# Splitting the first block's scan and preparing modulated weights as columns in a one-core adaLN layer kernel

## The chip, the cores and the metric

The kernel runs on one core of a Trainium2 chip. The metric is the device time of one execution in microseconds. Each version is timed in several runs, and one further execution is recorded by the hardware profiler. All arithmetic is in float32.

## The reference, cut to what matters

```python
# x: (4, 2048, 512); c: (4, 512)
mod = (silu(c) @ wmod).reshape(4, 6, 1, 512)
sa, ca, ga, sb, cb, gb = mod[:, 0], mod[:, 1], ..., mod[:, 5]
ga = sign(ga) * max(|ga|, 0.25); gb = sign(gb) * max(|gb|, 0.25)     # sign(0) = +1
h = layernorm(x) * (1 + ca) + sa
x = x + ga * attn(h)
h = layernorm(x) * (1 + cb) + sb
x = x + gb * ffn(h)

# attn(u): M = 64, state of 2M per batch, scanned over t
omega = clip(softplus(u @ W_omega.T + b_omega), 1e-4, 100)
zeta = sigmoid(u @ W_zeta.T + b_zeta)
A = omega**2; S = 1 / (1 + DT*DT*A); d = 1 - zeta; F = u @ W_B.T + b_B
z[t] = d*(S*z[t-1] - DT*A*S*y[t-1]) + F[:M];  y[t] = d*(DT*S*z[t-1] + S*y[t-1]) + F[M:]
attn = concat(z, y) @ C.T + u @ D_mat.T

# ffn(x): x_prev is x one step earlier in t, 0 at t = 0
r = sigmoid((mu_r*x + (1-mu_r)*x_prev) @ W_r.T)
k = relu((mu_k*x + (1-mu_k)*x_prev) @ W_k.T)**2
ffn = r * (k @ W_v.T)
```

## The kernel before, in words

**Units and blocks.** Time is cut into eight blocks `s` of `W` = 256 steps. A unit is one batch of one block, so there are 32 units, numbered block by block: unit `i` has `s, b = divmod(i, 4)`. The order of the instructions on each engine is the order of the Python calls (`tc.manual_schedule()`); every engine works its own queue in that order, and semaphores make it wait for the others.

**Gates.** For each unit, `load` brings natural x into two tiles `xs` (three buffers in all), `norm` computes the layer-norm statistics with VectorE's BN instructions (`tile_stats`, L104, L105, L129) and the inverse deviation `rs` with a power on GpSimd (POOL, L130). `send` writes `rs` to DRAM and `spread` reads it back over all partitions as `bc`; the first four units do this with a diagonal matrix and a matmul instead (`spread_now`, L148 to L150). `project` (L161) multiplies the transposed x by a gate weight into the single PSUM buffer `pg`, and `hand_over` multiplies by `bc` (L169) and writes the gate inputs with four ScalarE instructions (L174) into `pre` and `f`.

**Scan.** `scan(s)` returns a list of steps with costs for all four batches of a block: softening (softplus and sigmoid by Abs, Exp and Ln on ScalarE, L191 to L194, then L200 to L205 on VectorE), eight chunk steps, six joins in a tree, the falls back down, eight state steps, and `by_batch`, which reorders the states and sends them to the tile `y` (L309). The list is taken a few steps at a time by `take(budget)` between other work. A chunk step begins with copies on ScalarE (L221 to L223).

**Finish.** For each unit, `attend` multiplies transposed x by `dg` (L347) and the states by `cg` (L348), adds both to x on VectorE (L350, L351), takes statistics and normalizes into `xn` (L363). `mix` transposes `xn` on TensorE (L382) and forms the two time-shifted mixtures on ScalarE and VectorE (L388, L391, and L394 on POOL for the first column). `key` (L407), `receptance` (L421) and `value` (L431) are the three products of the second half, with their results in PSUM buffers of the tag `pm` (two of them). The transposes use the two buffers of the tag `pt`, and attend's products the three of `px`.

**The loop.** Pass `i` of the main loop runs `key(i)`, the statistics of unit `i + 9`, `attend(i + 1)`, `receptance(i)`, `mix(i + 1)`, the gate products of unit `i + 8` and `value(i)`, and takes scan steps of the next block in between. So the gates of the first eight units and the whole scan of block 0 lie ahead of the loop.

**What is prepared ahead of the loop.** The six rows of the modulation are products with four output rows (`mod_rows`, L488); five of them are transposed into columns by `mod_cols` (L500, L501). From them come: gate weights `wgb`, centred by a matmul (`shared_weights`, L512, L517); `dg`, the D weights times ga along the output (`d_gate`, on POOL, L526), centred and scaled by `d_centre` (L533, L537); `cg`, the C weights times ga (L621, POOL); the row `d0`, spread through DRAM (`d_rows`, L505, L506) and added to x on POOL (`shift`, L337); and `wvb`, the value weights scaled by gb on ScalarE and transposed on TensorE, 16 pieces of 128 by 512 (`value_weights`, L670, L673, L674).

Transfers are issued by SP, apart from some weight loads that stand in ScalarE's queue.

Of the kernel before, what the change touches and what calls it, by code (L numbers as in the profile page):

```python
# [32 lines left out]

class Unit:
# [9 lines left out]
def adaln_layer_kernel(ctx: ExitStack, tc: tile.TileContext, x, x_t, c_t, wmod, w_gate, w_b, b_gate, b_f, c_mat, d_mat,  # L44
                       w_r, w_k, w_v, mu_r, mu_k, out):
# [12 lines left out]

# [25 lines left out]
    omus = const.tile([P, 2, KC], F32, name="omus")  # L84
    ct = const.tile([P, KC, B], F32, name="ct")
# [10 lines left out]
    def load_transposed(u):  # L96
        t = p3.tile([P, KC, W], F32, tag="xt", name=f"xt_{u.tag}")
        for n in range(NT):
            nc.sync.dma_start(t[:, :, ts(n, P)], x_t[u.b, u.t0 // P + n])
        return t  # L100
# [6 lines left out]
    pre_of, f_of, y_of = {}, {}, {}  # L107

    class Gates:
# [13 lines left out]
        def norm(self):  # L123
# [8 lines left out]
        def send(self):  # L132
            self.row = dram.tile([W], F32, tag=f"st{self.u.tag}", name=f"st_{self.u.tag}")
            nc.sync.dma_start(self.row.rearrange("(n p) -> p n", p=P), self.r)

        def load_t(self):
            self.xt = load_transposed(self.u)

        def spread(self):
            self.bc = p2.tile([P, W], F32, tag="bc", name=f"bc_{self.u.tag}")  # L140
            nc.sync.dma_start(self.bc, self.row.unsqueeze(0).broadcast_to([P, W]))

        def spread_now(self, diag):
# [3 lines left out]
            for n in range(NT):  # L147
                nc.vector.tensor_scalar_mul(diag[:, ts(n, P)], ident, self.r[:, n : n + 1])  # L148
                nc.tensor.matmul(pb[:, ts(n, P)], ones, diag[:, ts(n, P)], start=True, stop=True)
            nc.scalar.copy(self.bc, pb)  # L150

        def project(self):
            u = self.u
            s, b = u.s, u.b
            if s not in pre_of:
                pre_of[s] = p2.tile([P, 2, L, Q, NCH], F32, tag="pre", name=f"pre_{s}")
                f_of[s] = p2.tile([P, 2, L, Q, NCH], F32, tag="f", name=f"f_{s}")
# [7 lines left out]
        def hand_over(self):  # L165
            u = self.u
            s, b = u.s, u.b
            g = p1.tile([P, 2, W], F32, tag="g", name=f"g_{u.tag}")
            nc.vector.tensor_mul(g, self.pg, self.bc.unsqueeze(1).broadcast_to([P, 2, W]))  # L169
            q, hs = b // 2, slice((b % 2) * M, (b % 2) * M + M)  # L170
            for i, dst in enumerate((pre_of[s], f_of[s])):
                for j in range(2):
                    src = slice(j * M, j * M + M)
                    nc.scalar.activation(  # L174
                        dst[hs, j, :, q, :].rearrange("p l c -> p c l"),
                        g[src, i, :].rearrange("p (c l) -> p c l", l=L),
                        AF.Identity,
                        bias=bias[src, i, b : b + 1],
                    )

    def scan(s):


        env = {}

        def soften_act():
            pre = env["pre"] = pre_of[s]
            env["f"] = f_of[s]
            o, z = (pre[:, j].rearrange("p l q c -> p (l q c)") for j in range(2))
            t = env["t"] = p1.tile([P, Q * W], F32, tag="soft", name=f"soft_{s}")  # L190
# [5 lines left out]
        def soften(lo, hi):  # L196

            pre, t = env["pre"], env["t"][:, lo:hi]
# [8 lines left out]
        def at(name, kind, l):  # L207
            return env[name][:, kind, l].rearrange("p q c -> p (q c)")

        def both(l):  # L210
            return env["f"][:, :, l].rearrange("p i q c -> p i (q c)")
# [3 lines left out]
        def chunk_step(l):  # L215


            new = p2.tile([P, 2, 3, QC], F32, tag="new", name=f"new_{s}_{l}")
            gl, al = at("pre", 0, l), at("pre", 1, l)
            if l == 0:  # L220
# [8 lines left out]
            uv = p1.tile([P, 2, 3, QC], F32, tag="uv", name=f"uv_{s}_{l}")  # L229
            gv = p1.tile([P, 3, QC], F32, tag="gv", name=f"gv_{s}_{l}")  # L230
# [3 lines left out]
                al.unsqueeze(1).broadcast_to([P, 6, QC]),  # L234
# [380 lines left out]
    for b in range(2):  # L615
        d_gate(b)
# [182 lines left out]
```

## Time and profile before

| quantity | value |
|---|---|
| median of 3 runs | 1261.17 us (1259.66 to 1262.08) |
| the profiled execution | 1261.01 us |
| its span, first to last instruction | 1259.2 us |
| mean granted TensorE clock | 0.958 |
| PE, PEld, DVE, ACT, POOL busy | 1160.7, 674.8, 752.0, 477.7, 174.4 us |
| share of the span in the chain that ended last: PE, DVE, ACT, DMA | 86%, 3%, 2%, 2% |

PE is TensorE's matmul, PEld its weight loads, DVE VectorE, ACT ScalarE, POOL GpSimd, SP the engine that issues most transfers. A float32 matmul is recorded as two passes: four matmuls into one tile stand as `x8`. The chain of waits is followed back from the last instruction: each piece of time is put down to the instruction that the next one had to wait for. The granted clock is the share of full speed that TensorE was given.

### The profile page before, as it was taken

To read this page: it belongs to the slowest core of one execution; us is meant where nothing else is said; L and a number is where in the kernel's file an instruction comes from. 1 tells how busy PE (TensorE), PEld (TensorE's weight loads), DVE (VectorE), ACT (ScalarE), POOL (GpSimd) and SP (SyncE) were. 2 spreads that over 40 slices of the span, in tenths; PEclk is the share of its full clock that TensorE was granted. 3 is DMA by queue.
4 is the path that set the end of the run, shared out by engine and by line. 5 is a ranking of instruction groups with operands and counts; after the bars stand their busy time and mean duration, and the time that the engine had idled before them with its cause. 6 is when DMAs were issued, how large, how long until landed. Compare 5 with 4: busy or idle time off the path is not lost.

```text
span 1259.2 us, 11785 instructions
## 1 busy us (share of the span) xinstructions
PE 1160.7 (92%) x3692; PEld 674.8 (54%) x3692; DVE 752.0 (60%) x2044; ACT 477.7 (38%) x796; POOL 174.4 (14%) x254
## 2 busy tenths in 40 slices
PE   6781475899999999999999999999999999999998
PEld 2621343456655566555665555665556665555554
DVE  2557513886488647874587538863886368743332
ACT  1331534333453345434533445334533453233232
POOL 0340001111101111111111111110111011111110
PEclk9895667899999999999999999999999999999999
DMA  8565423123333333233322232323232211121100
GB/s 266 194 118 93 74 67 79 39 80 88 104 89 88 88 87 85 88 89 96 89 81 68 75 95 80 88 88 105 88 89 71 67 50 51 51 67 50 50 18 33
DMA packets 120270, 105.95 MB, mean 84 GB/s; under 512 B 15880, under 2 KB 90120, under 8 KB 119952
## 3 DMA queue, kind: packets, MB, share of 16 engines
q1 hardware_dynamic: 116064, 101.27, 29.7%
q10 hardware_dynamic: 4144, 3.94, 1.0%
q8 instruction: 29, 0.48, 0.2%
q14 instruction: 33, 0.27, 0.1%
HBM read 84.16 MB, written 16.82 MB: 80 GB/s over the span
## 4 chain that ended last, share of the span: by engine, by line
PE 86%; DVE 3%; ACT 2%; DMA 2%; issue 1%; POOL 0%; SPq 0%; DVEq 0%; ACTq 0%
PE pk_c L407 18%; PE pr_c L421 18%; PE pv_c L431 17%; PE pd_c L347 17%; PE pg L161 8%; PE pc_c L348 4%; PE pt_c L382 2%; PE pwv L673 1%; DMA bc<-st 1%; DMA xs<-in_x_dram 1%; PE pdm L533 1%; ACT wvs L670 1%; ACT wvb L674 1%; ACT f L174 0%; ACT pre L174 0%
## 5 line engine op out<-in xcount | busy, mean ns | idle before, releaser
L407 PE MATMUL pk_c<-mixed_c,wk 128*128 128x256 f32 x1024 | 228.1, 381 | 12.9 <-POOL mixed_c L394 12.9
L347 PE MATMUL pd_c<-dg,xt 128*128 128x512 f32 x512 | 232.4, 597 | 0.0
L421 PE MATMUL pr_c<-wr,mixed_c 128*128 128x512 f32 x512 | 227.0, 596 | 0.0
L431 PE MATMUL pv_c<-wvb,act_c 128*128 128x512 f32 x512 | 225.0, 592 | 0.0
L407 PEld LDWEIGHTS pk_c<-mixed_c,wk 128*128 128x128 f32 x1024 | 195.7, 191 | 53.3 <-issue 14.8
L391 DVE SCALAR_TENSOR_TENSOR mixed_c<-pt_c,prev_f,mixed_c 128x255 f32<-128x255 f32 x256 | 118.1, 482 | 122.9 <-ACT mixed_c L388 122.9
L363 ACT ACTIVATE xn_c<-x,nmr_c,rstd_c 128x512 f32<-128x512 f32 x64 | 48.6, 805 | 334.6 <-POOL nmr_c L360 334.6
L421 PEld LDWEIGHTS pr_c<-wr,mixed_c 128*128 128x128 f32 x512 | 98.2, 192 | 123.9 <-issue 123.8
L347 PEld LDWEIGHTS pd_c<-dg,xt 128*128 128x128 f32 x512 | 98.1, 192 | 110.6 <-issue 108.8
L431 PEld LDWEIGHTS pv_c<-wvb,act_c 128*128 128x128 f32 x512 | 96.7, 190 | 108.9 <-issue 106.2
L350 DVE SCALAR_TENSOR_TENSOR x<-pd_c,rs,x 128x512 f32<-128x512 f32 x64 | 47.5, 743 | 169.0 <-PE pd_c L347 168.9
L161 PE MATMUL pg<-xt,wgb 128*128 128x256 f32 x512 | 121.0, 391 | 15.4 <-DVE g L169 15.4
L388 ACT ACTIVATE mixed_c<-pt_c,mod,now_f 128x256 f32<-128x256 f32 x256 | 130.4, 561 | 11.9 <-DVE mixed_c L391 5.6
L412 ACT ACTIVATE act_c<-pk_c 128x512 f32<-128x512 f32 x64 | 38.2, 597 | 202.2 <-PE pk_c L407 202.2
L161 PEld LDWEIGHTS pg<-xt,wgb 128*128 128x128 f32 x512 | 98.7, 197 | 29.1 <-DVE g L169 15.5
L433 DVE TENSOR_TENSOR r_c<-pv_c,r_c 128x512 f32<-128x512 f32 x64 | 44.2, 690 | 90.8 <-PE pv_c L431 88.8
L359 POOL TENSOR_TENSOR rstd_c<-rstd_c,neg_half 128x2 f32<-128x2 f32 x32 | 24.6, 769 | 515.9 <-DVE nmr_c L358 515.9
L174 ACT ACTIVATE pre<-g,bias 64x256 f32<-64x256 f32 x64 | 46.8, 731 | 84.8 <-DVE g L169 84.3
L337 POOL TENSOR_TENSOR x<-x,d 128x1024 f32<-128x1024 f32 x32 | 75.6, 2362 | 2.0 <-DMA x<-in_x_dram 2.0
L348 PE MATMUL pc_c<-cg,y 128*128 128x512 f32 x128 | 66.4, 601 | 4.8 <-DVE x L350 4.8
L130 POOL TENSOR_TENSOR rs<-var,neg_half 128x2 f32<-128x2 f32 x32 | 24.9, 779 | 306.8 <-DVE var L129 292.1
L423 ACT ACTIVATE r_c<-pr_c 128x512 f32<-128x512 f32 x64 | 36.9, 588 | 51.1 <-PE pr_c L421 51.0
(119 smaller groups left out, 1029.6 us busy)
## 6 DMA issues: line engine op xcount, KB each, us to landing
xt<-in_x_t_dram SPq DMA_DIRECT2D x128, 256.0 KB, 4.6
xs<-in_x_dram SPq DMA_DIRECT2D x64, 256.0 KB, 4.6
x<-in_x_dram SPq DMA_DIRECT2D x32, 512.0 KB, 4.0
out_dram<-r_c SPq DMA_DIRECT2D x64, 256.0 KB, 2.1
wvb<-in_wmod_dram SPq DMA_DIRECT2D x5, 1024.0 KB, 9.5
y<-pre SPq DMA_DIRECT2D x64, 64.0 KB, 2.0
bc<-st SPq DMA_DIRECT2D x28, 128.0 KB, 4.7
wvb<-in_wmod_dram SPq DMA_DIRECT2D x4, 256.0 KB, 4.7
```

Of the source, the lines that this page charges most:

```text
L161: nc.tensor.matmul(self.pg[:, i, :], wgb[:, b, k, ts(i, P)], self.xt[:, k, :], start=(k == 0), stop=(k == KC - 1))
L174: nc.scalar.activation(dst[hs, j, :, q, :].rearrange("p l c -> p c l"), g[src, i, :].rearrange("p (c l) -> p c l", l=L), AF.Identity, bias ...
L337: nc.gpsimd.tensor_tensor(xt, xt, d0[:, self.u.b, :].unsqueeze(1).broadcast_to([P, NT, D]), ALU.add)
L347: nc.tensor.matmul(pd, h[:, k, ts(n, P)], dg[:, b, k, :], start=(k == 0), stop=(k == KC - 1))
L348: nc.tensor.matmul(pc, y_of[u.s][:, b, ts(n, P)], cg[:, b, :], start=True, stop=True)
L350: nc.vector.scalar_tensor_tensor(xt[:, n, :], pd, r, xt[:, n, :], ALU.mult, ALU.add)
L363: nc.scalar.activation(self.xn[:, n, :], xt[:, n, :], AF.Identity, bias=nmr[:, n : n + 1], scale=rstd[:, n : n + 1])
L388: nc.scalar.activation(m, pt, AF.Identity, bias=mod[:, 2, k, b : b + 1], scale=now_f[:, b, i, k : k + 1])
L391: nc.vector.scalar_tensor_tensor(m[:, 1:], pt[:, : W - 1], prev_f[:, b, i, k : k + 1], m[:, 1:], ALU.mult, ALU.add)
L407: nc.tensor.matmul(pk[:, j, :], wk[:, k, ts(2 * e + j, P)], mixed[:, 1, k, :], start=(k == 0), stop=(k == KC - 1),)
L421: nc.tensor.matmul(pr, mixed[:, 0, k, ts(n, P)], wr[:, k, :], start=(k == 0), stop=(k == KC - 1))
L431: nc.tensor.matmul(pv, act[:, k, ts(n, P)], wvb[:, u.b, k, :], start=(k == 0), stop=(k == KC - 1))
```

## The change

Block 0 is scanned in two parts, batches 0 and 1 first and batches 2 and 3 later; `part` gives each its half of `pre` and `f`, and `scan(0, 0)` and `scan(0, 1)` are two lists with instructions of half the width. The other blocks are scanned as before. The order ahead of the loop and in its first four passes is written anew: the loop now starts with five units' gates done, and the gates of units 5 to 11 are computed in passes 0 to 3. The five modulation vectors after ca come directly as columns (`mod_cols`, 16 small matmuls). D is loaded in its natural layout and scaled in three places: `d_scaled` multiplies it by the ca row on VectorE, `Turn.rows` by the ga column on ScalarE with the centring as a bias, and `Turn.turn` transposes it on TensorE, with copies back by `keep`. C and the value weights take the same way. The statistics of the units from 2 on are two accumulating ScalarE instructions per tile, and units 2 to 7 send and spread `rs` from POOL's queue. For block 0, `d0` is added inside the states' PSUM group by a matmul that picks the row (`states`). The first units' x is loaded once for Gates and Finish, and free weight tiles hold it meanwhile. In pass 3 receptance and value come ahead of the next unit's attend.

```diff
+    def part(s, q):
+        if s not in parts_of:
...
+            if s == 0:
+                n = 2 * L * NCH
+                parts_of[s] = [Part(s, h, 1, pre[:, ts(h, n)], f[:, ts(h, n)]) for h in range(Q)]
+            else:
+                parts_of[s] = [Part(s, 0, Q, pre, f)] * Q
+        return parts_of[s][q]
-        def norm(self):
+        def norm_dve(self):
...
+        def norm(self, junk=False):
...
+                nc.scalar.activation(t, src, AF.Identity, scale=-1.0 / D, accum_out=mean[:, n : n + 1])
...
+                nc.scalar.activation(
+                    t, src if junk else t, AF.Square, scale=1.0 if junk else -float(D), bias=mean[:, n : n + 1],
+                    accum_out=var[:, n : n + 1],
+                )
+            nc.gpsimd.tensor_scalar(var, var, 1.0 / D, EPS, ALU.mult, ALU.add)
+            nc.gpsimd.tensor_tensor(self.r, var, neg_half, ALU.pow)
-        def hand_over(self):
+        def multiply(self):
+            self.g = p1.tile([P, 2, W], F32, tag="g", name=f"g_{self.u.tag}")
+            nc.vector.tensor_mul(self.g, self.pg, self.bc.unsqueeze(1).broadcast_to([P, 2, W]))
+        def deliver(self, share=False):
...
+                    if share and i == 1:
+                        nc.vector.tensor_scalar_add(there, here, bias[src, i, b : b + 1])
+                    else:
+                        nc.scalar.activation(there, here, AF.Identity, bias=bias[src, i, b : b + 1])
-    def scan(s):
+    def scan(s, q=0):
+        to = part(s, q)
...
+        def states(self, n):
+            pc = ps3.tile([P, D], F32, tag="px", name=f"pc_{self.tag}_{n}")
+            if self.row is not None:
+                pick = ident[:B, u.b : u.b + 1].broadcast_to([B, P])
+                nc.tensor.matmul(pc, pick, self.row, start=True, stop=False)
+            nc.tensor.matmul(pc, y_of[u.s][:, u.b, ts(n, P)], cg[:, u.b, :], start=(self.row is None), stop=True)
...
+    def mod_cols(wm, name):
+        pt = ps2.tile([P, KC, B], F32, tag="pt", name=name)
+        for e in range(KC):
+            for k in range(KC):
+                nc.tensor.matmul(pt[:, e, :], wm[:, k, ts(e, P)], st[:, k, :], start=(k == 0), stop=(k == KC - 1))
+        return pt
+    def d_scaled(b):
+        pc = ps3.tile([P, D], F32, tag="px", name=f"pca{b}")
+        pick(pc, carow[:B, :], b)
+        nc.vector.tensor_mul(dg[:, b], dn, pc.unsqueeze(1).broadcast_to([P, KC, D]))
+    class Turn:
+        def rows(self):
+            for e in range(KC):
...
+                    nc.scalar.activation(
+                        a, self.src[:, e, :], AF.Identity, scale=self.scale[:, e, b : b + 1],
+                        bias=self.shift[:, e, b : b + 1],
+                    )
+        def turn(self):
+            self.pts = [
+                ps2.tile([P, D], F32, tag="pt" if k < 2 else "pm", name=f"turn_{self.name}{self.b}_{k}")
+                for k in range(KC)
+            ]
+            for k, pt in enumerate(self.pts):
+                for e in range(KC):
+                    nc.tensor.transpose(pt[:, ts(e, P)], self.dst[:, e, ts(k, P)], ident)
+        def keep(self):
+            for k, pt in enumerate(self.pts):
+                nc.scalar.copy(self.dst[:, k, :], pt)
+    weights_to(dn, d_mat, nc.scalar)
+    weights_to(dt, d_t, nc.scalar)
+    weights_to(cn, c_mat, nc.scalar)
+    weights_to(wn, w_v, nc.scalar)
...
+    gts[1].deliver(share=True)
+    side += scan(0, 0)
+    take(0.1)
+    d_scaled(0)
+    d_scaled(1)
+    take(3.4)
...
+    shared_weights(3, pws[1])
+    fin[0].add_products()
+    turn_v[0].rows()
+    turn_d[1].turn()
+    turn_d[1].keep()
+    turn_c[1].turn()
+    turn_c[1].keep()
+    d_scaled(2)
+    fin[0].attend(lambda: None)
+    gts[2].project()
...
+    fin[0].mix(lambda: None)
+    gts[4].project()
+    turn_v[0].turn()
+    gts[3].deliver()
+    side += scan(0, 1)
+    take(0.1)
+    turn_v[0].keep()
+    gts[4].multiply()
+    gts[4].deliver()
+    gts[6].norm()
...
+        if i == 0:
+            gates(5)
+            gts[6].spread(nc.gpsimd)
+            gts[7].norm()
+            gts[7].send(nc.gpsimd)
+            gts[8].load()
+            gts[8].norm()
+            gts[8].send()
+            turns = [turn_d[2], turn_c[2]]
+        if i == 1:
+            take(1)
+            gates(7)
...
+            turns = [turn_d[3], turn_c[3], turn_v[1]]
+        if i == 2:
+            gates(9)
+            fin[4].load()
+            turns = [turn_v[2]]
+        for t in turns:
+            t.rows()
...
+        if late:
+            take(1)
+            f.receptance()
+            turn_v[3].turn()
+            turn_v[3].keep()
+            ahead.products()
+            gates(11)
+            ahead.add_products()
+            f.value(lambda: None)
+            ahead.attend(lambda: None)
+            ahead.mix(fin[i + 2].shift)
...
+            if ahead:
+                ahead.attend(lambda: take(a2))
+            if i == 1:
+                side += scan(1)
+                take(0.1)
+            take(b_)
+            for t in turns:
+                t.turn()
+                t.keep()
+            f.receptance()
```

## The prediction

> **What bounds the kernel now.** I read the busy rows of the page first, then the windows by stage, then the chain of waits, then the timeline at the places where the chain leaves TensorE.
>
> ```profile
> PE   6781475899999999999999999999999999999998
> PEclk9895667899999999999999999999999999999999
> 0.00:36.58 36.58, 24.29 (x84) 10.98 (x84) 9.68 (x31) 3.52 (x6) 2.10 (x8) 0.95 0.86 283
> 91.99:162.80 70.81, 22.71 (x84) 16.54 (x84) 43.66 (x149) 24.62 (x42) 7.08 (x16) 0.60 0.44 74
> 204.57:251.58 47.01, 42.20 (x117) 23.86 (x118) 32.70 (x78) 15.61 (x28) 7.36 (x9) 0.89 0.28 75
> 285.13:318.68 33.55, 33.55 (x109) 19.83 (x109) 19.93 (x60) 13.91 (x24) 4.52 (x7) 1.00 0.32 83
> ```
>
> In the PE row only the first eight slices are not full. In a window the columns are length, then busy time of PE, PEld, DVE, ACT and POOL, then granted clock, DMA share and GB/s. From the second pass on, PE is busy 33.55 of 33.55 us: nothing is to be had there unless TensorE gets less work. The loss is all ahead of that.
>
> ```profile
> 204.57 8.90 PE pk_c L407 x32
> 251.58 6.91 PE pk_c L407 x32
> 285.13 6.91 PE pk_c L407 x32
> 318.68 6.91 PE pk_c L407 x32
> 352.23 6.91 PE pk_c L407 x32
> ```
>
> These are the starts of key(0) to key(4) in the chain. After key(4) both versions have the same work left (gates of units 12 on, passes 4 to 31), so I ask one thing: when does key(4) start? The gain is 352.23 minus that.
>
> ```profile
> 36.58 0.68 DVE L169 TENSOR_TENSOR g<-pg,bc 128x512 f32<-128x512 f32 x1
> 67.94 1.28 ACT L192 ACT_TABLE_LOAD   x1
> 69.24 0.63 ACT L192 ACTIVATE soft<-soft 128x512 f32<-128x512 f32 x1
> 90.01 0.69 DVE L104 BATCH_NORM_STATS2 stats_a<-xs 128x6 f32<-128x512 f32 x1 [10.79 <-DMA xs<-in_x_dram]
> 91.99 0.41 DVE L200 SCALAR_TENSOR_TENSOR pre<-pre,soft 128x256 f32<-128x256 f32 x1
> 162.80 5.01 SPq L309 DMA_DIRECT2D y<-pre  x8
> 172.90 5.83 PE L347 MATMUL pd_c<-dg,xt 128*128 128x512 f32 x8
> 204.57 8.90 PE L407 MATMUL pk_c<-mixed_c,wk 128*128 128x256 f32 x32 [12.93 <-POOL mixed_c L394]
> ```
>
> First gate product 36.58, first softening on VectorE 91.99 (after four gates and a 10.79 us wait for xs), states sent 162.80, key(0) 204.57. The eight pd_c passes took 5.83 us there, 3.43 in the steady chain: a cold start, 2.4 us.
>
> **The change, by stages up to key(4).** Durations are rows of before. (a) *To the first product.* mod_rows (3.43 us at full clock) becomes mod_cols: 32 passes with 4 columns; L601 did 16 such passes in 1.84 us, so 3.7: no gain each. But only two pw (1.99 each) and one mod stand ahead: pw to 17.8, wgb to 19.4, diagonal and its matmul 20.7, psa 24.5, bias matmuls 26.7, pg 3.7, so product at 30.5 (was 36.58). ScalarE issues four weight loads here and stays behind their queue slots until about 25 (the first window moves 283 GB/s; some 6.5 MB stand up to the D load, 23 us); its next work, bc, is needed only at 30: cost 0, up to 6 if that cover is gone.
>
> (b) *To softening.* Gate 1: 35.5. Its f half on VectorE: no row; bounds 0.29 (a plain 128x256 tensor_scalar) and 0.74 (the strided twin on ScalarE), taken 0.4 each. Two d_scaled, 128x2048: four L351 rows make 2.8, without their starts 2.1; taken 2.3. Softening at 40.8 (was 91.99). It no longer waits for gates 2 and 3, for centring or for xs.
>
> (c) *To the states.* Softening 3.7; gate columns seven small ones, 1.4: 46.0. The first chunk step then waits for three copies on ScalarE behind D rows (four L670 rows at 0.70) and C rows (4 x 0.29): 50.5. Half-width steps: 1.31 for 1.85 (128x192 0.36, 128x96 0.26 and so on); seven of them and two small copies 60.0; joins 3.0, start 0.8, five falls 3.1, eight state steps at 0.98 (was 1.18), gb 1.0: 75.7. States are sent at 76.4 (was 162.80). ScalarE's statistics of units 2 to 4 (eight and four L413-like rows of 0.63) and TensorE's column products lie beside it.
>
> (d) *To key(0).* VectorE wgb and products 4.8 (80.5); ScalarE copy, statistics 5, V rows, first keep 83.0; turned C and pick, cold, 85.7; d_scaled 2.3; attend sums to 92.0; POOL 0.95, xn 1.6, gates 3, pick and transposes to 99.9; mixed to 105.5. Then a **new wait**: turn_v[0] takes both "pm" PSUM buffers, and ScalarE empties them only after deliver(3) 2.95, softening 4.0 with two table loads, and three keeps 1.7: key(0) at 113.7 (was 204.57). Behind key(0) on TensorE stands gate 5, and VectorE's product 5 stands ahead of the second scan, which so starts at 126.8.
>
> (e) *Pass 0, 61.2 us (was 47.0).* Key cold 8.9, gate 5 3.45, product 0.7; ScalarE deliver 2.95, statistics 7 and 8 5.1, wait for xs of unit 8 about 3 (its buffer is freed inside statistics 7, landing 4.6), D and C rows 4.0, copies 0.6: 142.6. VectorE step, first tile, step, second tile 7.5; POOL and xn 2.5; D keeps 1.7: 154.3, when receptance gets its buffer; cold 9.1, transposes 1.0, gate 6 3.5, value 6.9: key(1) at 174.9.
>
> (f) *Pass 1, 65.3 (was 33.55).* The second scan ends at 189.0, its states land 193.6 (four issues 0.63 apart, 2.0 us landing); attend cold to 202.3; sums, POOL, xn 4.4, softening of block 1 5.0, eight keeps 4.5: 216.2; receptance cold 9.1, four d0 picks 3.4, transposes 1.1, gate 8 3.5, value 6.9: key(2) at 240.2 (was 285.13).
>
> (g) *Pass 2, 50.0.* Key and gate 9 10.4; product, four full steps, tile, step, tile 15.0; POOL and xn 2.5, keeps 1.7; receptance cold 8.9, transposes, gate, value 11.5: key(3) at 290.2. (h) *Pass 3, 48.6.* Scan of block 1 ends 304.8, copies and sigmoid 3.2, turns 0.6, products 6.9, gate 11, value, states 12.1; then with TensorE empty sums 3.2, POOL 1.0, xn 1.5, transposes 1.1, half of mixed 2.4, a cold start 2: key(4) at 338.8.
>
> **Sum:** 352.23 - 338.8 = 13.4. The profiled execution took 1261.01 us with a span of 1259.2, 0.16 under the median of the runs, 1261.17. 1261.0 - 13.4 = 1247.6, say 1248.
>
> **Costed at nothing.** In the steady passes 1.9 us of VectorE (two L104, two L105, L129) become 2.55 of ScalarE, which is busy 13.91 of 33.55; it runs under the 8.6 us of attend products. Uncovered it would cost 2.55 x 20 units = 51. An accumulating ACTIVATE has no row: at least the plain 0.63, at most one more small instruction (0.22) each; I take the plain one, 20 on the chain, so up to 4. The st and bc transfers of units 2 to 7 move from SP's queue to POOL's, which SP's loads no longer stand behind; before showed 8.0 and 4.7 us to landing on SP. On POOL they may be some us later or earlier; unit 6 has 40 us to spare, unit 4 about 4. On SP the two bounces of ga and d0 through DRAM (L505, L506) and 2.5 MB of second loads for block 0 go, and 1 MB of D transposed comes. W_k and W_r move from ScalarE's queue to SP's: W_k stands ahead of nothing needed before 60 us, W_r is issued at about 101 and is first read at 154. Transposed x of units 4 to 7 now goes into wvb, so these issues wait on SP for the sb and gb columns (about 55 and 65), with only xs of unit 5 and the y transfers (76) behind them: 11 us of cover, and each us beyond it is a us of key(0). What POOL loses is large: D and C products of 2391 ns x8 and 1288 x4, and their contention; no gain counted beyond the stages.
>
> **Two rules that speak against it.** Pass (d) to (f) put transposes where the centring matmuls were. The Trainium skill, TensorE: Matmul & The Clock Gate (Part 4: PE-mode transpose; Why this matters for your kernels), says that transposes do not count as TensorE activity for its clock, and that gaps of some 3 us bring half rate. The pd_c row agrees: it began slow right after 16 us of transposes. With its 2.4 at most I put some 14 us of cold starts into (d) to (h); by the page, half of a 3.4 us window, 1.7 each, they would be 12. The other rule, ScalarE: Activation LUTs (What ACT_TABLE_LOAD costs), charges 2.66 us for a switch; here the load at 67.94 was over in 1.28 and the next instruction began at 69.24. Four loads on the chain would cost 5.5 more by the page; I keep the trace's.
>
> **Rivals.** *A, the queues close up.* Passes 0 to 3 hold only 165 us of TensorE work at full clock (4 x 30.1, seven gates 24.2, 88 transposes 11.4, ten picks 8.6) against my 225. If a third of the 60 us of waits and cold starts is not there, key(4) is at 319 and the time 1228. For it: I let every wait end last in full. Against: the queues are in order and the buffers few. *B, TensorE stays cold* (slower). Place: passes 0 to 2, 129 us of work at full clock, 142 with my cold starts, a mean clock of 0.91. The windows of before had 0.60 to 0.70 where PE was half busy, and 0.89 at 42.20 of 47.01. At 0.80 the 129 become 161: 19 more, time 1267. It turns slower once the clock of these passes is below about 0.83 and the stretch lies on the chain. Against: most of the waits there are for ScalarE, and some stretch hides under them. *C, statistics* of 1.4 us instead of 0.63 on ScalarE would eat the gain; nothing near that is in the trace.
>
> **How the numbers follow.** Forecast 0.54 (1248, own range 1236 to 1260); A 0.18 (1228); B 0.24 (1267); C 0.04 (1265). The measurement tells 0.2%, 2.5 us, from no change. Forecast, about seven eighths, and A are faster: 0.65; the rest of the forecast and the lower edge of B are the same: 0.09; slower 0.26. The range reaches from the lower side of A to the upper of B, 1224 to 1271.
>
> **What would show it.** Right: first product near 30, states sent near 76, key(0) near 114 ended by ScalarE's keep and not by POOL, key(2) near 240 and key(4) near 339, then 33.55 us per pass. Wrong: a steady pass above 33.6 (statistics uncovered); a clock under 0.83 in passes 0 to 2 (B); L178 or L180 above 0.85 us (C); first product after 36 (loads hold ScalarE).

## The result, and the profile after

The changed kernel takes 1265.71 us (median of 7 runs, 1261.14 to 1269.88) against 1261.17 for the kernel before on the same chip (7 runs, 1259.66 to 1262.59): ratio 1.0033, 95% interval 1.001 to 1.0056. The forecast was a gain of 13 us; it lost 4.5. Its profiled execution took 1264.29 us with a span of 1262.3, 1.4 under its median.

The busy rows of the page after, in 40 slices of 31.6 us:

```profile
PE   6998688789889999999999999999999999999998
...
PEclk8677888898989999999999999999999999999999
```

PE is fuller at the start than before, and its clock lower in the first three slices (8, 6, 7 for 9, 8, 9), higher in the four behind them. The windows of the changed kernel by the stages of the forecast (length; busy PE, PEld, DVE, ACT, POOL; clock; DMA share; GB/s):

```profile
0.00:37.04 37.04, 26.61 (x99) 18.94 (x100) 8.56 (x30) 3.94 (x6) 2.09 (x8) 0.82 0.99 321
37.04:47.66 10.62, 10.21 (x58) 8.08 (x57) 7.56 (x8) 6.88 (x13) 0.00 (x0) 0.95 0.65 240
47.66:89.74 42.08, 41.17 (x184) 35.33 (x185) 28.27 (x139) 19.71 (x49) 9.14 (x25) 0.65 0.52 107
89.74:131.18 41.44, 28.61 (x106) 17.57 (x104) 17.59 (x32) 25.05 (x46) 4.34 (x10) 0.80 0.44 70
131.18:189.62 58.44, 47.91 (x148) 29.03 (x149) 24.64 (x77) 36.08 (x75) 7.02 (x15) 0.85 0.15 37
189.62:256.89 67.27, 53.74 (x173) 31.84 (x172) 33.06 (x115) 40.02 (x73) 3.21 (x9) 0.87 0.26 67
```

The third row is the odd one. TensorE is busy 41.17 of 42.08 us, yet its granted clock is 0.65. The timeline of the changed kernel shows the work (start, length, instruction, times; in brackets the idle time ahead of it and who ended it):

```profile
21.12 5.37 PE L617 MATMUL psa<-st,wvb 128*128 128x4 f32 x32
26.75 3.57 PE L752 MATMUL pbias<-mod,wraw 128*128 128x4 f32 x16 [0.27 <-DVE mod L742]
30.19 6.75 PE L218 MATMUL pg<-xt,wgb 128*128 128x256 f32 x16
37.04 0.69 DVE L224 TENSOR_TENSOR g<-pg,bc 128x512 f32<-128x512 f32 x1 [6.12 <-PE pg L218]
...
47.25 6.97 PE L617 MATMUL pga<-st,wvb 128*128 128x4 f32 x32
54.07 6.97 PE L617 MATMUL pcb<-st,wvb 128*128 128x4 f32 x32
54.25 0.17 DVE L623 TENSOR_SCALAR sgna<-pga 128x16 f32<-128x16 f32 x1 [2.81 <-PE pga L617]
72.76 0.17 DVE L805 COPY mod<-psb 128x16 f32<-128x16 f32 x1 [3.62 <-PE psb L617]
79.27 3.63 PE L617 MATMUL pgb<-st,wvb 128*128 128x4 f32 x32
131.18 9.20 PE L513 MATMUL pk_c<-mixed_c,wk 128*128 128x256 f32 x32 [6.15 <-ACT wvb L684]
```

One vector of 32 passes with 4 columns takes 3.63 at 79.27, 113 ns a pass, and 6.97 at 47.25 and 54.07, 218 ns. The first is the price the forecast used for all five. The gate product at 30.19 takes 6.75 where the next one takes 3.72. TensorE does not idle in either; it works at half clock, as the windows over these instructions show (the gate product, the cb vector, the gb vector):

```profile
30.19:36.80 6.61, 6.61 (x18) 5.30 (x19) 0.56 (x3) 0.00 (x0) 0.00 (x0) 0.53 1.09 356
54.07:61.00 6.93, 6.93 (x34) 6.93 (x35) 2.19 (x13) 4.47 (x11) 1.05 (x3) 0.50 0.55 28
79.30:82.80 3.50, 3.50 (x35) 3.50 (x33) 3.05 (x18) 3.33 (x10) 0.02 (x1) 1.00 0.01 2
```

Against the forecast, from the start of the span:

| | before | forecast | after |
|---|---|---|---|
| first gate product | 36.58 | 30.5 | 37.04 |
| first softening on VectorE | 91.99 | 40.8 | 47.66 |
| states sent | 162.80 | 76.4 | 89.74 |
| key(0) | 204.57 | 113.7 | 131.18 |
| key(1) | 251.58 | 174.9 | 189.62 |
| key(2) | 285.13 | 240.2 | 256.89 |
| key(3) | 318.68 | 290.2 | 307.49 |
| key(4) | 352.23 | 338.8 | 352.61 |

In this trace all of the miss lies ahead of key(0): 6.5 us to the first product, 6.5 from the softening to the states (42.1 for 35.6), 4.1 from there to key(0). The four passes took 221.4 for 225.1. At key(4) the kernels are level; key(4) begins at half clock behind a wait of 2.10 us for POOL (it takes 9.44 for 7.07), so that key(5) is 2.9 us late (388.69 against 385.79), and that is nearly all of the 3.1 by which the span is longer.

Executions differ. The run e6_stats below has the same instructions up to pass 3. In its trace the sb vector ran mostly at full clock, VectorE did not wait for it, and the stage from the softening to the states was shorter, 39.43 for 42.08:

```profile
47.36:86.79 39.43, 38.58 (x184) 32.51 (x184) 28.22 (x139) 19.72 (x49) 9.16 (x25) 0.67 0.56 115
65.86 3.91 PE L619 MATMUL psb<-st,wvb 128*128 128x4 f32 x32
```

Its key(0) starts at 127.26 and its key(3) at 301.38, 3.9 and 6.1 us ahead of the trace above, with nothing changed. So a difference of a few us between two single traces shows no effect of an edit by itself; there the medians and their intervals decide.

### The profile page after: what moved, and what is told of

Same layout as the page of the kernel before. It is cut to its first block, busy times and chain, and to the rows that moved or that the text cites. A ratio compares the mean times of both kernels' runs of the same rounds, so it can differ in the third digit from the quotient of the medians.

```text
span 1262.3 us, 12427 instructions
## 1 busy us (share of the span) xinstructions
PE 1194.8 (95%) x3896; PEld 716.6 (57%) x3896; DVE 703.7 (56%) x2000; ACT 583.9 (46%) x1092; POOL 153.5 (12%) x282
## 4 chain that ended last, share of the span: by engine, by line
PE 72%; issue 0%; DVE 0%; POOL 0%; DVEq 0%; POOLq 0%
PE pk_c L513 16%; PE pv_c L537 15%; PE pr_c L527 15%; PE pd_c L420 15%; PE pg L218 5%; PE pc_c L446 4%; PE pt_c L488 2%; DVE r_c L539 0%; DVE r_c L540 0%; POOL mixed_c L500 0%; POOL edge_c L480 0%; DVEq L539 0%; POOLq L413 0%
## 5 line engine op out<-in xcount | busy, mean ns | idle before, releaser
L513 PE MATMUL pk_c<-mixed_c,wk 128*128 128x256 f32 x1024 | 231.3, 384 | 9.7 <-ACT wvb L684 6.1
L469 ACT ACTIVATE xn_c<-x,nmr_c,rstd_c 128x512 f32<-128x512 f32 x64 | 48.6, 806 | 270.5 <-POOL nmr_c L466 270.5
L218 PE MATMUL pg<-xt,wgb 128*128 128x256 f32 x448 | 106.9, 394 | 1.2 <-DVE g L224 1.2
L218 PEld LDWEIGHTS pg<-xt,wgb 128*128 128x128 f32 x448 | 87.2, 199 | 15.0 <-DVE g L224 1.8
L446 PE MATMUL pc_c<-cg,y 128*128 128x512 f32 x128 | 69.8, 630 | 3.1 <-DMA y<-pre 3.1
L413 POOL TENSOR_TENSOR x<-x,d 128x1024 f32<-128x1024 f32 x28 | 65.9, 2355 | 0.0
L184 POOL TENSOR_SCALAR var<-var 128x2 f32<-128x2 f32 x30 | 5.8, 192 | 431.9 <-ACT xs L180 411.1
```

The source lines that it names most:

```text
L218: nc.tensor.matmul(self.pg[:, i, :], wgb[:, b, k, ts(i, P)], self.xt[:, k, :], start=(k == 0), stop=(k == KC - 1))
L413: nc.gpsimd.tensor_tensor(xt, xt, d0[:, self.u.b, :].unsqueeze(1).broadcast_to([P, NT, D]), ALU.add)
L446: nc.tensor.matmul(pc, y_of[u.s][:, u.b, ts(n, P)], cg[:, u.b, :], start=(self.row is None), stop=True)
L469: nc.scalar.activation(self.xn[:, n, :], xt[:, n, :], AF.Identity, bias=nmr[:, n : n + 1], scale=rstd[:, n : n + 1])
L513: nc.tensor.matmul(pk[:, j, :], wk[:, k, ts(2 * e + j, P)], mixed[:, 1, k, :], start=(k == 0), stop=(k == KC - 1),)
```

## The experiments

Times below are medians; as the kernel before itself differs between chips (1258.5 to 1261.2), each comes with its ratio to before on the same chip and the 95% interval. The changed kernel's is 1.0033 (1.001 to 1.0056).

**The columns by themselves** (into the kernel before, where TensorE is warm and busy throughout):

```diff
         f.key()
+        if i == 8:
+            for r in range(3):
...
+                for e in range(KC):
+                    for k in range(KC):
+                        nc.tensor.matmul(
+                            pt[:, e, :], wk[:, k, ts(e, P)], st[:, k, :], start=(k == 0), stop=(k == KC - 1)
+                        )
+        if i == 14:
+            for r in range(3):
...
+                for k in range(KC):
+                    nc.tensor.matmul(pr[:B, :], st[:, k, :], wk[:, k, :], start=(k == 0), stop=(k == KC - 1))
```

> The kernel before, with added products that nobody reads in two passes of its steady loop, where TensorE is busy throughout and at full clock: in pass 8, behind key, three vectors of 32 passes of 4 columns each (weights 128x128); in pass 14, behind key, the same three products as rows, 8 passes of 512 columns each. Theory 'columns leave TensorE at half clock by themselves': the first vector takes about 3.7, the later ones 7.0 each, 16 to 18 in all, the granted clock of that stretch falls to 0.5 to 0.7, and the product behind them is slow for some us; the rows take 10.3 to 10.8 at clock 1.0. Rival 'it is the start of the kernel' (loads, TensorE not yet warm): three vectors in 11 at clock 1.0.

One run took 1288.13. The windows of this kernel over the columns (three rows), the product behind them, and the rows:

```profile
490.78:494.00 3.22, 3.22 (x31) 3.22 (x29) 3.05 (x7) 1.71 (x5) 0.00 (x0) 1.00 0.40 130
494.00:495.00 1.00, 1.00 (x10) 1.00 (x9) 0.64 (x1) 0.00 (x0) 0.00 (x0) 0.88 0.00 0
495.00:507.48 12.48, 12.48 (x60) 12.48 (x60) 0.00 (x0) 0.00 (x0) 0.00 (x0) 0.50 0.02 1
507.48:511.50 4.02, 4.02 (x6) 1.83 (x7) 0.00 (x0) 0.00 (x0) 0.00 (x0) 0.50 0.00 0
711.10:721.60 10.50, 10.50 (x26) 2.08 (x25) 0.00 (x0) 1.23 (x2) 0.00 (x0) 1.00 0.12 37
```

```profile
507.48 5.83 PE L347 MATMUL pd_c<-dg,xt 128*128 128x512 f32 x8
...
721.52 3.70 PE L347 MATMUL pd_c<-dg,xt 128*128 128x512 f32 x8
```

The 96 column passes take 16.70 us (490.78 to 507.48), and the product behind them 5.83 instead of 3.70; the rows take 10.50 at clock 1.00. TensorE is full in every row of the columns, yet its clock is 1.00 for 3.2 us, 0.88 in the next one, and 0.50 from there on: it fell some 4.0 us after the columns began, and stayed at half for 4 us of the wide product behind. In the changed kernel the gb vector began at full clock and was over in 3.63, inside such a time. So neither the start of the kernel nor its loads (DMA share 0.02 over the 12.48 us of columns at half clock) are needed: column products let the clock fall by themselves. Whether it is their few columns or a weight load for every pass, no run separates.

**The sa vector as a row** (e1_sa_row):

```diff
...
+    def turned(pr, name):
+        nc.vector.tensor_copy(mrow[:B, :], pr[:B, :])
+        pt = ps2.tile([P, KC, B], F32, tag="pt", name=name)
+        for k in range(KC):
+            nc.tensor.transpose(pt[:, k, :], mrow[:B, ts(k, P)], ident[:B, :B])
+        return pt
...
-    nc.vector.tensor_copy(mod[:, SA], mod_cols(wm_sa, "psa"))
+    nc.vector.tensor_copy(mod[:, SA], turned(mod_rows(wm_sa, "psa"), "psa"))
```

> The changed kernel with the sa columns made by rows: 8 passes of 512 columns into 4 rows, a VectorE copy and four small transposes, in place of 32 passes of 4 columns. Theory 'columns leave TensorE at half clock': rows take 3.4, copy and turning 1.0, the bias products 1.8 to 2.5 and gate product 0 3.7, so VectorE's first gate product starts near 31.5 instead of 37.04, and the whole is 2 to 5 us shorter than the changed kernel's 1265.7. Rival 'the loads hold it' (DMA share 0.99 until 37): TensorE waits for data, gate product 0 stays at 6.7 and the first gate product at 36 to 38, the whole unchanged.

1260.59, ratio 1.0014 (1.0002 to 1.0026). Its timeline:

```profile
20.86 3.60 PE L625 MATMUL psa_rows<-wvb,st 128*4 128x512 f32 x8
25.90 1.95 PE L767 MATMUL pbias<-mod,wraw 128*128 128x4 f32 x16 [0.27 <-DVE mod L757]
27.70 5.39 PE L218 MATMUL pg<-xt,wgb 128*128 128x256 f32 x16
33.20 0.69 DVE L224 TENSOR_TENSOR g<-pg,bc 128x512 f32<-128x512 f32 x1 [4.25 <-PE pg L218]
```

The gate product comes 3.8 us earlier. The rival had it unchanged. Half clock still begins inside the gate product, behind the 16 small bias passes and 1.0 us of idle, so the 31.5 was not reached. Over all runs the first product lies at 35.5 to 37.0 with sa as columns and nothing added (7 traces), at 32.3 to 33.6 with rows (six traces), and at 36.1 in a seventh (e15_rows_after), whose bias and gate product ran slow again. So the gain at this place is some 3 us. In the whole it isn't clear of noise: the interval overlaps the changed kernel's, and key(0), at 126.49, lies as e6_stats has it (127.26) with sa as columns.

Columns are not the only thing that lowers the clock at the start. In three traces (e2_rows, e15_rows_after, e16_no_wait_c) sa's row product itself took 5.29 instead of 3.60, and in the kernel before one of its row products did, behind a wait for its weights. e2_rows, then the kernel before:

```profile
20.15 5.29 PE L625 MATMUL psa_rows<-wvb,st 128*4 128x512 f32 x8
...
16.82 5.29 PE L488 MATMUL pmod<-wvb,st 128*4 128x512 f32 x8 [3.48 <-DMA wvb<-in_wmod_dram]
```

TensorE also stands idle there for 1.95 us shortly ahead of sa's product, in the changed kernel and in e2_rows. That such gaps share in the fall is likely and was not tested.

**Wide matmuls between the columns** (e3_warm):

```diff
                 nc.tensor.matmul(pt[:, e, :], wm[:, k, ts(e, P)], st[:, k, :], start=(k == 0), stop=(k == KC - 1))
+            keep_warm(name, e)
...
+    def keep_warm(name, e):
+        for i in range(2):
...
+            nc.tensor.matmul(keep_warm.to, zeros[:, :P], zeros, start=True, stop=True)
```

> The changed kernel with all columns as they are and work added: two wide bf16 matmuls of zeros (128x512, read by nobody) behind every 8 passes of 4 columns, 8 for each vector, and 4 in the bias products; about 0.22 each at full clock, so 1.7 per vector. Theory 'columns leave TensorE at half clock': the added work shortens it: a vector takes about 5.3 with its added work instead of 7.0, gate product 0 takes 3.7 instead of 6.75, first gate product near 33.5. Rival 'a column product costs its weight loads at any clock': it adds 1.7 to each vector and first gate product goes to 39 or later.

1273.22, ratio 1.0123 (1.0103 to 1.0142); the rival's first gate product after 39 came in, at 39.99.

```profile
26.63 1.71 PE L626 MATMUL psa<-st,wvb 128*128 128x4 f32 x8
28.19 1.01 PE L619 MATMUL warm_psa<-zeros 128*128 128x512 bf16 x2
```

Eight passes still take 1.71, 214 ns each. This dose did not hold the clock, so it is no remedy. The rival's reason, one price at any clock, does not hold either: gb's eight passes took 0.95 in this run, at clock 1.00. As to the cause, the products added to the loop decide, where the same product was made by columns and by rows.

**A quarter of the later columns** (e17_cols_cut; the kernel leaves out three quarters of the products for ga, cb and sb):

```diff
-            for k in range(KC):
+            ks = range(KC) if name in ("psa", "pgb") else range(1)
+            for k in ks:
...
```

> The changed kernel with a quarter of the products for ga, cb and sb (8 passes of 32, the others left out, so that these three vectors are not the reference's), and nothing else. It takes 72 passes of 4 columns from TensorE, 15.7 us at the 218 ns of each in the changed kernel. Theory 'TensorE under these columns is the bound from the softening to the states': states sent near 79 (89.7), key(0) 6 us or more ahead of 131.2, the whole 4 to 7 us under 1265.7. Rival 'VectorE's scan is the chain there': states sent no earlier than 86, the whole within 2 us of 1265.7.

1257.56, ratio 0.9988 (0.9982 to 0.9995), clear of the changed kernel's. The stage from softening to states:

```profile
46.12:81.68 35.56, 29.48 (x117) 21.82 (x118) 28.19 (x139) 19.73 (x49) 9.17 (x25) 0.65 0.45 126
```

35.56 us long, with the same VectorE work (28.19; 28.27 in the changed kernel): the forecast's 35.6 for this stage. Key(0) is at 123.79, 7.4 us ahead of the changed kernel's trace and 3.5 ahead of that of e6_stats. The columns' time in this stage is what the forecast had at nothing. The clock did not come back with them gone: it is 0.65 here too, and it had already fallen in pmean, 32 passes of 8 columns ahead of the stage (0.68 from 41.81 to 47.00). So this run shows what the passes cost at half clock, not what lowered it.

**Waits taken from VectorE there, one after the other.** First the chunk steps ahead of ga's columns (e8_chunk_first), then sb's copy three steps later too (e13_c_waits). Comments in this cut and the next ones name the run or the old place:

```diff
+    take(1.0)                        # e8: chunk steps 0 and 1
     gate_cols(ga, pt, "a")
...
-    nc.vector.tensor_copy(mod[:, SB], pt)
...
+    take(3.1)                        # e13
+    nc.vector.tensor_copy(mod[:, SB], psb)
```

> The changed kernel with the first scan's chunk steps 0 and 1 taken ahead of the ga columns and of D's and C's scaling on ScalarE; VectorE waited there 2.8 us for the ga product and 4.35 us for ScalarE's copies. Theory 'these waits are on the chain to the states': states sent 4 to 7 us ahead of 89.7, key(0) 3 us or more ahead of 131.2, the whole near 1261. Rival 'TensorE at half clock decides this stage' (turned D, psb, the shared products): states sent 0 to 3 us earlier, key(0) within 1 us of 131.2, the whole within 2 us of 1265.7.

> The changed kernel with the first chunk steps ahead of ga (as label e8_chunk_first) and VectorE's copy of the sb columns three chunk steps later, nothing else. Theory 'late next': taking out the waits for ga and for ScalarE only brought VectorE to the wait for the sb columns (4.1 there); with that gone too, states sent near 84 (89.7 and 88.6) and the whole 3 to 5 us under the changed kernel, near 1261. Rival 'what is sent earlier waits for TensorE' (key(0)'s wait for ScalarE's copies): states near 84, the whole within 1.5 us of 1265.7.

1262.89, ratio 1.0013 (1.0 to 1.0027), and 1262.05, 1.0007 (0.9996 to 1.0019); both intervals overlap the changed kernel's. States went at 88.55 and 86.94: the rival of the first, and 2.9 us short for the second (e6_stats, without either edit, has 86.79). Where the time stayed, first in e8_chunk_first, then in e13_c_waits:

```profile
60.96 0.17 DVE L794 TENSOR_SCALAR mod<-pcb 128x16 f32<-128x16 f32 x1 [4.35 <-PE pcb L617]
...
71.55 0.17 DVE L806 COPY mod<-psb 128x16 f32<-128x16 f32 x1 [4.09 <-PE psb L617]
```

```profile
80.49 0.17 DVE L623 TENSOR_SCALAR sgnb<-pgb 128x16 f32<-128x16 f32 x1 [2.10 <-PE pgb L617]
```

Each wait taken away brought VectorE to the next vector that TensorE still had in hand (cb and sb, then cb again, 4.37, and gb).

**Rows for all four vectors**, in two orders (e2_rows, e15_rows_after), and the second order on the version of the queue moves below (e14_rows_best):

```diff
-    pt = mod_cols(wm_cb, "pcb")
+    pcb = mod_rows(wm_cb, "pcb")
...
+    pt = turned(pcb, "pcb")          # e2: ahead of turn_d[0]; e15, e14: behind it
     nc.vector.tensor_scalar_add(mod[:, CB], pt, 1.0)
```

> The changed kernel with the columns of sa, ga, cb and sb made by rows and small transposes; gb stays as columns, since its 32 passes took 3.63 at full clock. Theory 'columns leave TensorE at half clock': first gate product near 31.5 (37.04), softening on VectorE near 42 (47.7), states sent near 79 (89.7), key(0) near 121 (131.2), and the whole about 1256. Rival 'the queues behind absorb it' (VectorE waits for ScalarE's statistics and D rows, and key(0) for ScalarE's keeps): states sent no earlier than 86, the whole above 1262.

> The changed kernel with sa, ga, cb and sb by rows in the same better order, and no other edit. In label e2_rows TensorE stood 5.5 us for cb's turning. Theory 'the columns cost the whole miss ahead of the loop': states sent near 80 (89.7), key(0) near 121 (131.2), the whole near 1256. Rival 'only sa's columns count' (the later ones lie beside VectorE's scan): states sent near 85, the whole near 1260.6, as label e1_sa_row.

> As label e11_queues, with ga, cb and sb also made by rows, and each row copied and turned behind the work that waits: ga's product ahead of pmean, cb's turning behind turn_d[0], sb's behind the shared products. Theory 'half clock was what the stage from the softening to the states still cost': TensorE has 10 us less there, states sent near 81 (86.05), the whole near 1243. Rival 'VectorE's own scan steps are now the chain' (some 35 us of them): states sent no earlier than 84.5, the whole within 2 us of 1246.9.

1265.66, ratio 1.0055 (1.0037 to 1.0072); 1264.44, 1.0044 (1.0027 to 1.0061); 1249.54, 0.9928 (0.9913 to 0.9942), against 0.9897 without the rows. None of the theories: states went at 88.35, 94.50 and 93.54. The timeline of e15_rows_after:

```profile
69.66 0.17 DVE L813 TENSOR_SCALAR mod<-pcb 128x16 f32<-128x16 f32 x1 [9.02 <-PE pcb L632]
...
76.91 0.56 PE L632 MATMUL psb<-ident,mrow 4*128 4x4 f32 x4 [6.71 <-DVE mrow L629]
```

A row goes from TensorE to VectorE and back to TensorE, and each trip stands behind whatever that queue holds. These three runs say nothing of the columns' price; they show that a cheaper product with two hand-overs can cost more.

**The later waits.** The early turn of the value weights (e4_turn_early), and pass 0 with the second scan's first steps ahead of gate 5 (e5_pass0):

```diff
     turn_c[1].keep()
+    turn_v[0].turn()                 # e4: from behind project(4)
+    turn_v[0].keep()                 # e4: from behind the softening
...
         if i == 0:
-            gates(5)
+            gts[5].project()         # e5
+            take(4.0)
+            gts[5].multiply()
+            gts[5].deliver()
...
```

> The changed kernel with turn_v[0] and its three copies on ScalarE moved ahead, behind turn_c[1]: then key(0) no longer waits for PSUM buffers that ScalarE empties behind delivery 3 and the softening. Theory 'the wait is on the chain': key(0) near 125 (131.18), key(1) 5 to 6 earlier, the whole near 1260. Rival 'VectorE's second scan is late next' (it starts behind gate product 5, and ScalarE's statistics hold its first chunk step): key(0) is earlier, key(2) at most 2 us earlier than 256.9, the whole above 1263.

> The changed kernel with pass 0 reordered: the second scan's softening and first two chunk steps are taken right behind gate product 5 on TensorE, ahead of its multiplication on VectorE and its delivery and the statistics of units 7 and 8 on ScalarE. VectorE waited there 17.8 us for gate product 5 and 10.7 us for ScalarE's copies of the first chunk step. Theory 'the second scan is on the chain of passes 0 and 1': its states go out 8 to 12 us ahead of 204.9 and key(2) starts 5 us or more ahead of 256.9, the whole near 1260. Rival 'TensorE and ScalarE set the passes': what moves ahead is taken from attend(1), key(1) comes later than 189.6 by some us, key(2) within 2 us of 256.9, the whole within 2 us of 1265.7.

1260.27, ratio 1.0005 (0.9991 to 1.0019), and 1254.15, 0.9943 (0.9928 to 0.9958). e4 brought key(0) to 118.39, 12.8 us earlier, twice what was expected: with its PSUM free, key starts on the first half of mixed; and from 90 to 118 the granted clock was 0.94 instead of 0.76. But key(1), at 184.19, kept 5.4 of it, and 1.5 against e6_stats (185.73); in the whole e4's interval overlaps the changed kernel's. The rest went to this wait for the second scan's first copies, behind the statistics of units 7 and 8 (timeline of e4_turn_early):

```profile
152.28 0.36 DVE L296 TENSOR_TENSOR uv<-new,pre 128x192 f32<-128x192 f32 x1 [17.38 <-ACT new L288]
```

That wait, 10.70 in the changed kernel, is what e5 attacks: the second scan's states go at 193.36 (204.89, and 200.98 in e6_stats), key(2) starts at 249.31 (256.89 and 252.30), and the whole is clear of the changed kernel's interval. The theory holds; the wait was on the chain.

**Statistics back on VectorE from unit 12 on** (e6_stats):

```diff
         def norm(self, junk=False):
+            if self.u.s >= 3:
+                return self.norm_dve()
```

> The changed kernel with the statistics of units 12 to 31 back on VectorE (two BN instructions for each tile in place of four accumulating ScalarE ones), that is, in the passes from 3 on only. Theory 'statistics on ScalarE are hidden' (the prediction's cost at nothing): pass length stays 33.55 from key(5) on, the whole within 1 us of the changed kernel's 1265.7. Rival 'they cost in the steady passes': 0.1 us or more for each of 20 units, the whole 2 to 5 us shorter.

1263.83, ratio 1.0018 (1.0004 to 1.0031), no difference from the changed kernel's that the intervals tell. A steady window of the changed kernel, then of e6_stats:

```profile
400.00:700.00 300.00, 300.00 (x969) 177.51 (x968) 187.81 (x536) 147.57 (x277) 42.27 (x71) 1.00 0.31 87
```

```profile
400.00:700.00 300.00, 300.00 (x969) 177.54 (x968) 201.51 (x573) 125.35 (x208) 41.22 (x63) 1.00 0.30 86
```

The work moves between DVE and ACT, PE stays full at the same 969 passes: hidden in both.

**The edits together.** sa as a row, e4, e5 and e8 at once (e9_all); then sb's copy later and attend(0) ahead of turn_v[0] and D's scaling for batch 2 (e11_queues); then gate product 0 ahead of sa (e12_best); and, on e11_queues, hardly a wait for columns during the first scan (e16_no_wait_c; 1.10 for ga is left):

```diff
+    gts[0].project()                              # e12 only: ahead of the sa rows
...
-    pt = mod_cols(wm_cb, "pcb")
+    pcb = mod_cols(wm_cb, "pcb", px=True)         # e16: another PSUM tag
...
     take(3.1)
+    nc.vector.tensor_scalar_add(mod[:, CB], pcb, 1.0)
     nc.vector.tensor_copy(mod[:, SB], psb)
...
-    gate_cols(gb, pt, "b")
     take(100)
+    gate_cols(gb, pt, "b")
```

> The changed kernel with four edits at once: sa by rows, the early turn and copies of turn_v[0], pass 0 reordered, and the first chunk steps ahead of ga. If the delays add up, each on the chain: first gate product near 33, states sent near 80, key(0) near 109, and the whole near 1246, faster than the kernel before by 1%. Rival 'one chain stands behind the other' (what one edit gives, the next only uncovers): the whole no better than the best of them alone, near 1259.

> The four edits together (label e9_all), and two more moves in the queues: VectorE's copy of the sb columns comes three chunk steps later, and attend(0) comes ahead of turn_v[0] and of D's scaling for batch 2. In the four edits VectorE waited 4.1 us for the sb columns (TensorE at half clock) where the waits for ga and for ScalarE had been taken out. Theory 'the sb columns were late next': states sent near 81 (85.2), key(0) near 113 (119.8), the whole near 1245. Rival 'TensorE's own queue sets the states' (shared products and D's turning at half clock): states sent within 1 us of 85, the whole near 1249.

> As label e11_queues, and gate product 0 on TensorE ahead of the sa rows and the bias products, which only its delivery needs. Theory 'the start is a chain through TensorE': both gate products delivered near 36 instead of 38.5, the whole 1 to 3 us shorter than e11_queues, about 1243. Rival 'ScalarE and the ga columns come next': no difference beyond 1 us.

> As label e11_queues, and VectorE no longer waits for columns during the first scan: the cb product goes to another PSUM buffer and its column is added late, beside sb's, and the gb columns follow the state steps. In e11_queues VectorE waited 4.4 us for cb and 4.6 for gb there, while TensorE was busy 41.3 of the 42.1 us. Theory 'TensorE at half clock is the bound of this stage': states sent 6 to 9 us ahead of 86.05, but key(0) not more than 2 us ahead of 115.45 and the whole within 1.5 us of 1246.9. Rival 'VectorE's waits are the bound': key(0) 5 us or more earlier, the whole near 1241.

| | time | ratio to before | states sent | key(0) |
|---|---|---|---|---|
| e9_all | 1249.96 | 0.9908 (0.9893 to 0.9923) | 85.16 | 119.80 |
| e11_queues | 1246.92 | 0.9897 (0.9879 to 0.9915) | 86.05 | 115.45 |
| e12_best | 1247.61 | 0.9899 (0.9885 to 0.9914) | 86.89 | 116.29 |
| e16_no_wait_c | 1237.58 | 0.9834 (0.9808 to 0.986) | 78.65 | 106.12 |

e9's parts add up in the main, less at key(0) than expected, since the attend behind the early turn ran at half clock. e11's move of sb's copy only found the next vector: VectorE now stood 4.64 us for gb, and states did not go earlier. Key(0) came 4.4 us earlier, which leaves attend(0) as its source; in the whole the two intervals overlap. e12 gave nothing: gate product 0 took 3.62, but product 1 then ran slow (5.25) and was multiplied at 38.74 for 37.89. e16 beats both kernels, by 1.7% of the kernel before, and went against the theory that I put first: TensorE stays busy 35.01 of 35.76 us, and still its vectors cost nothing there once VectorE does not stand for them.

```profile
42.89:78.65 35.76, 35.01 (x177) 31.57 (x178) 29.61 (x142) 19.61 (x49) 8.90 (x25) 0.65 0.52 118
78.65:106.12 27.47, 27.12 (x118) 17.75 (x116) 13.92 (x22) 16.88 (x33) 4.16 (x9) 1.00 0.42 58
```

The clock in the first row is 0.65 as in the changed kernel, the length 35.76 instead of 42.08.

## Why the prediction was wrong

The step that failed is the price of mod_cols in (a), "L601 did 16 such passes in 1.84 us, so 3.7: no gain each". That row stood in a warm stretch; a vector measured 5.4 to 7.0 in four of five places. With it fell what stands around it, the overlap in (c) above all:

- *(a)* the bias passes (3.57 for 1.84) and the gate product (6.75 for 3.7) behind the columns. With 1.7 + 1.7 + 3.0 the three make 6.4 of the 6.5 us. Rows for sa gave back about 3 of them in six traces of seven. What lowers the clock there is shown in part: columns can, but rows in this place also began at half clock in three traces.
- *(c)* "TensorE's column products lie beside it". They do, but their results are awaited inside the scan. At 7.0 each, with pmean (4.05, which the sum left out), they came late for VectorE: its waits, 2.81 for ga and 3.62 for sb, make 6.4 of the stage's miss of 6.5. Two edits put it back to 35.56 (columns cut) and 35.76 (waits gone), against the forecast's 35.6, both with the clock still at 0.65; so it is the waits for the late columns that lengthen the stage.
- *(d)* attend and gates at clock 0.80: the states' products took 2.07 each (1.12 at full clock), gate product 2 took 4.47. Only the turned C and the pick were taken cold there. How the clock falls in (d) was not isolated: with turn_v[0] moved ahead of attend(0) it was 0.94 in e4 but 0.75 in e9, and with turn_v[0] right behind gate product 2 it was 0.88 in e11, e12 and e14 and 1.00 in e16.

In the whole, cutting the columns gave back 0.45% (5.7 us) of the changed kernel, and taking away VectorE's waits gave e16 0.63% (7.9 us) over e11; both are clear of the intervals. Sa's row gave 0.19%, which is not. Single traces do not settle the shares: key(3) starts at 301.50 with sa's row, at 301.12 with the columns cut, and at 301.38 in e6_stats, which changes nothing up to there. So the cost in (c) is shown by runs of its own; the shares of (a), (d) and key(4) in the miss of 18 us are read from one trace.

What held. The new wait of key(0) for ScalarE's copies was there (6.15 us), VectorE's wait for gate 5 too. Passes 0 to 3 came to 58.4, 67.3, 50.6 and 45.1 for 61.2, 65.3, 50.0 and 48.6. d_scaled took 2.25 (2.3), the f half 0.45 (0.4). The steady pass is 33.55 with the statistics on ScalarE; a unit's statistics take 2.73 ahead of the loop (49.77 to 52.50) for the 2.55 taken; each accumulating ACTIVATE is followed by a separate read of 0.19. ScalarE was free at 25.8, as said, and nobody waited. The issues into the value weights' tiles ended at 85.0, 4.7 us ahead of the states, so that cover held too. ACT_TABLE_LOAD kept the trace's 1.28.

Of the rivals, A did not come, nor C: a statistic took 0.68 (2.73 for four), and e6_stats shows them hidden in the steady passes. B named the right mechanism in the wrong place: TensorE at half clock, but its clock in passes 0 to 2 was 0.85 to 0.93, above the 0.83 that would have decided, and the price was paid in (a), (c) and (d). That its 1267 lies near the measured 1265.7 is luck. The sign "first product after 36 (loads hold ScalarE)" fired for another reason: bc was there at 26.2, and the product waited for TensorE. Two rows of before were read too lightly. Its own row product at 16.82 took 5.29, so that the start could have been known as a cold place. The slow pd_c row, read as agreeing with the rule on transposes, stood behind transposes with 1.3 to 4.2 us of idle time between the groups of four; it does not tell transposes from gaps. I weighed the clock rule for the transposes only; the chances for B should have covered every stage in which the change puts narrow products on TensorE.

## What to carry to other kernels

Price a TensorE instruction by the clock it will run at, not only by a row of its shape: many passes of few columns, each with its own weight load, keep TensorE busy and yet bring its clock to half, and then what stands behind them pays as well. Work that is beside the chain is free only if nothing on the chain reads its result early: place the copy of such a result as late as its next reader allows, and look for the next wait of the same kind before measuring. Before a product is made cheaper by an added hand-over between two in-order queues, count what each queue holds ahead of the hand-over.

## What the runs showed of the hardware that was not expected

- Passes of 4 columns with 128x128 weights take 113 ns at full clock and 218 at half. In the warm loop the clock held for about 4.0 us of them (1.00 for 3.22 us, 0.88 over the next 1.00) and then fell to 0.50, with TensorE never idle. Two 128x512 bf16 matmuls behind every eight did not keep it up.
- The clock that an instruction meets differs between executions. The same 32 passes for sb took 6.99 us in the changed kernel's trace and 3.91 in that of e6_stats. The runs of the changed kernel spread over 8.7 us, those of before on the same chip over 2.9; that the clock makes this spread is not shown. The Trainium skill, TensorE: Matmul & The Clock Gate (Part 1: The HAM clock gate), says that the clock follows a window of activity that runs freely and does not start anew with the kernel, which would make such a spread; no run here shows the window.
